# Zero borders in the background, pool waits tile by tile, a finer start of the first group, and NCA in longer pieces

## The chip, the core and the metric

The kernel runs on one core of a Trainium2 chip. A core has TensorE for matmuls (PE in the profile, with its weight loads as PEld), VectorE (DVE), ScalarE (ACT), GpSimd (POOL) and SyncE (SP); the last one only issues DMA transfers here, and ScalarE issues some too. Each engine works through its own instructions in a fixed order. The metric is the device time of one execution in microseconds.

## The reference, cut to what matters

The input x is 32 images of 8 channels and 256 x 256 points, in fp32. Two layers follow, each with a residual.

```python
# layer 0: on z = groupnorm(x), 4 groups of 2 channels
grid = z
for _ in range(15):                                  # the lattice
    mapped = 3.9 * grid * (1 - grid)
    grid = 0.85 * (0.7 * mapped + 0.3 * conv3x3_per_channel(mapped)) + 0.15 * z
cml = clip(grid, 1e-4, 1 - 1e-4)
nca = sigmoid(conv1x1(relu(conv3x3(z, 8 -> 128)), 128 -> 8))
g   = sigmoid(conv1x1(relu(conv3x3(concat(z, cml, nca), 24 -> 8))))
x   = x + g * cml + (1 - g) * nca
# layer 1: y = groupnorm(x); x = x + conv3x3 of y and the weights, both quantised to whole numbers up to 127;
# the scale of y is its largest magnitude over the whole batch
```

The lattice is a chain of 15 convolutions on one channel: a step needs the step before it, with the neighbouring rows. The quantisation of layer one needs all of layer zero, so the two layers can't overlap.

## The kernel before, in words

**Stages.** Layer zero is done in eight groups of four images (GB = 4, so NG = 8). Four kinds of work exist in it:

- *Preparation* (`normalise`): loads x by pairs of channels, takes means and variances, writes the normalised values to DRAM in two layouts: `xq_s` for the lattice, and `xp_s` for NCA, as a high and a low part (`hi`, `lo`). One tile is one image and one pair of channels (512 KB). The staging tiles `xq`, `hi` and `lo` exist once, so a tile waits until the stores of the one before it have read them.
- *Lattice* (`lattice`): one unit is one channel of the four images of a group, in two streams of two images. A unit has 15 steps, a step three tiles, a tile six matmuls (L486). After a tile VectorE computes L494 and L499 for each stream. After the second and third tile, two small DMAs (`exchange`, L449 and L450) carry edge rows of `m_a` to their neighbours, for the next step.
- *NCA* (`nca`): per image nine block pairs in two parts each, and a short rest. A part has four or three rounds of 12 matmuls into `ph` (L563), which ScalarE turns into `h` (L573); the products of `h` with the second weights (L580) are made one part later. Each part's input rows `im` are loaded one part ahead.
- *Gate* (`gate`): combines the results for an image of the group before and writes `y_s`.

**Order.** TensorE's order is written out by hand. The lattice is the main line: `together` lets it emit one step, and then emits filler (NCA, gate, preparation) until the filler's share has caught up. A piece of filler is what lies between two `yield`s, and the number given to `yield` is its weight in microseconds; a step weighs 5.91. The weights of whole stages are `T_NCA, T_GATE, T_PREP, T_LATTICE = 520.0, 340.0, 34.0, 8 * 45 * 1.97`. So filler is never cut within a piece, and the lattice never within a step. The other engines' orders are chosen by a planner that takes the program order as priority.

**DMA queues.** Nearly all transfers are issued from SP, in one fixed order. `background(n)` issues up to n waiting transfers of a list (`later`) after each lattice tile: the loads of the next unit and the stores of finished ones. Zero borders (rows above and below the images in `xp_s`, `cm_s`, `nc_s` and `y_s`) are written from ScalarE's queue in the preparation part, L199 and L202, from a zero tile `zt`.

**Memory.** The preparation part uses pools of its own for weights and for `zt`. The pools of layer zero (`xp` for the tiles of x, `hp` for `h`, and so on) take the same memory after them. A pool waits for all users of the memory that it takes over.

**The start.** `prep(0, (0,))` prepares two of the four channel groups for all four images of the first group ahead of the lattice, the other two as filler ahead of NCA.

Of the kernel before, what the change touches and what calls it, by code (L numbers as in the profile page):

```python
# [40 lines left out]
P = 128  # L41
# [72 lines left out]
def kernel(  # L114
# [19 lines left out]
    def dram_ap(t, offset, dims):  # L134
        return bass.AP(t.tensor, t.offset + offset, dims)
# [17 lines left out]
    qw = cp.tile([P, 3, P], BF16, name="qw")  # L153
    wp_hi = cp.tile([P, 3, HID], F32R, name="wp_hi")
    wp_lo = cp.tile([P, 3, HID], F32R, name="wp_lo")
    wu_z = cp.tile([HID, 56], F32, name="wu_z")
    bp_sb = cp.tile([P, 1], F32, name="bp_sb")
    bv = cp.tile([P, 4], F32, name="bv")
# [13 lines left out]
    with tc.tile_pool(name="prep", bufs=1) as pp, tc.tile_pool(name="prep2", bufs=2) as pp2:  # L172
# [18 lines left out]
        nc.sync.dma_start(bv, bvec)  # L191


        zt = pp.tile([P, PW], F32, name="zt")
        G.memset(zt, 0.0)
        for t, n, w in (
            *((t, 2 * C, PW) for t in xp_s), *((t, C, W) for t in (*cm_s, *nc_s, *y_s))
        ):
            nc.scalar.dma_start(dram_ap(t, 0, [[w, n], [1, w]]), zt[:n, :w])  # L199
            for i in range(0, 11, 5):  # L200
                m = min(5, 11 - i) * n
                nc.scalar.dma_start(dram_ap(t, (257 + i) * n * w, [[w, m], [1, w]]), zt[:m, :w])  # L202

        V.tensor_copy(masks, kt[:, K_MASK : K_MASK + 4])
        V.tensor_copy(junk, kt[:, K_JUNK : K_JUNK + 2])
# [51 lines left out]
    with ExitStack() as one:  # L257

        one.enter_context(tc.manual_schedule(engines={mybir.EngineType.PE}))
        pool = lambda name, bufs, **kw: one.enter_context(tc.tile_pool(name=name, bufs=bufs, **kw))  # L260
        xp, sp2, gp, bp2, st = pool("xp", 4), pool("sp2", 1), pool("gp", 3), pool("bp2", 2), pool("st", 2)
        imp, hp, wk, wk1, np_ = pool("imp", 3), pool("hp", 12), pool("wk", 2), pool("wk1", 1), pool("np", 1)
# [25 lines left out]
        def normalise(jobs):  # L288

            def begin(b, half):
# [3 lines left out]
                for i in range(2):  # L297
                    g = 2 * half + i
                    xr = xp.tile([P, 2, 2, W], F32, name="xr", tag="xr")
                    nc.sync.dma_start(  # L300
                        xr.rearrange("p c h w -> p (c h) w"),
                        dram_ap(x, (b * C + 2 * g) * H * W, [[W, P], [P * W, 4], [1, W]]),
                    )
                    for j in range(2):
                        V.bn_stats(stats[:, i, j, :], xr[:, j].rearrange("p h w -> p (h w)"))
                    V.bn_aggr(mv[:, i, :], stats[:, i].rearrange("p j s -> p (j s)"))
                    xrs.append(xr)
                return b, half, xrs, mv

            def scale(b, half, xrs, mv):  # L310
                gs = slice(2 * half, 2 * half + 2)
                pm = ps_c.tile([P, 512], F32, name="pm", tag="pt")
                T.matmul(pm[:, 0:2], avg, mv[:, :, 0], start=True, stop=True)
                m, rstd = mean_x[:, b, gs], rstd_x[:, b, gs]
                V.tensor_copy(m, pm[:, 0:2])
                e = st.tile([P, 2], F32, name="e", tag="e")
                V.tensor_tensor(e, mv[:, :, 0], m, ALU.subtract)
                V.tensor_tensor(e, e, e, ALU.mult)
                V.tensor_tensor(e, e, mv[:, :, 1], ALU.add)
                return e  # L320

            def end(b, half, xrs, e):
                pv = ps_c.tile([P, 512], F32, name="pv", tag="pt")
                T.matmul(pv[:, 0:2], avg, e, start=True, stop=True)
                rstd = rstd_x[:, b, 2 * half : 2 * half + 2]
                V.tensor_scalar(rstd, pv[:, 0:2], GN_EPS, None, ALU.add)
                G.tensor_tensor(rstd, rstd, mhalf[:, 0:2], ALU.pow)
                for i, xr in enumerate(xrs):
                    g = 2 * half + i
                    flat = xr.rearrange("p c h w -> p (c h w)")  # L330
                    V.tensor_scalar(
                        flat, flat, mean_x[:, b, g : g + 1], rstd_x[:, b, g : g + 1],
                        ALU.subtract, ALU.mult,
                    )
                    xq = sp2.tile([P, 2, 2, 4, NJ], F32, name="xq", tag="xq")
                    S.activation(
                        xq.rearrange("p c h q j -> p (c h) q j"),
                        xr.rearrange("p c h (j q) -> p (c h) q j", q=4),
                        AF.Copy,
                    )  # L340
                    inner = lambda t: t[:, :, :, 1 : 1 + W]
                    V.tensor_copy(inner(hi), xr)
                    G.tensor_tensor(inner(lo), xr, inner(hi).bitcast(F32), ALU.subtract)
                    for h in range(2):
                        nc.sync.dma_start(
                            dram_ap(
                                xq_s[b % NBUF], (2 * g * H + P * h) * W, [[W, P], [H * W, 2], [1, W]]
                            ),
                            xq[:, :, h].rearrange("p c q j -> p c (q j)"),
                        )  # L350
                        for j, src in enumerate((hi, lo)):
                            nc.sync.dma_start(
                                dram_ap(
                                    xp_s[b % NBUF],
                                    (1 + P * h) * ROW + (C * j + 2 * g) * PW,
                                    [[ROW, P], [PW, 2], [1, PW]],
                                ),
                                src.bitcast(F32)[:, :, h, :],
                            )
                    yield 1.0  # L360
                ready.add((b, half))
# [14 lines left out]
        def lattice(g):  # L376


            def load(u):


                c, out, dmas = u % C, [], []
                assert all((u // C * GB + i, c // 4) in ready for i in range(GB))
                for s in range(2):
                    i = (2 * u + s) % 4
                    da, db = d_a[i], d_b[i]
# [72 lines left out]
            for c in range(C):  # L459
                u = g * C + c  # L460
                ds = units[u]
                for step in range(STEPS):
# [5 lines left out]
                    for i, ts in enumerate(tiles):  # L468
# [46 lines left out]
                        if step == STEPS - 1 and u + 1 in units:  # L515
                            begin(units[u + 1], ts)

                        background(len(later) if (c, step, i) == (C - 1, STEPS - 1, 2) else 3)
                    yield 5.91

        ROWS = ((2, 4, 10, 12, 3, 5, 11, 13), (1, 6, 8, 14, 7, 9))
# [31 lines left out]
        def nca(b):  # L553
# [57 lines left out]
            for p in range(9):  # L611
                for part in range(2):
# [22 lines left out]
            if (b + 1, 0) in ready and (b + 1, 1) in ready:  # L635
                loaded[b + 1] = rows(b + 1, 0, 0)
            two = hidden([im[64 * q : 64 * q + 48, 0, :2, :] for q in range(2)])
            yield 1.4
# [225 lines left out]
        for _ in prep(0, (0,)):  # L864
            pass
        for g in range(NG):
            fill, t = images(nca, g), T_NCA
            if g:
                fill, t = both(fill, t, images(gate, g - 1), T_GATE), t + T_GATE
            if g + 1 < NG:  # L870
                fill, t = both(fill, t, prep(g + 1, (0, 1)), T_PREP), t + T_PREP
# [104 lines left out]
```

## Time and profile before

| | |
|---|---|
| time, median of 3 | 14845.17 us (14838.8 to 14852.71) |
| profiled execution | 14861.1 us, mean TensorE clock 0.946 |
| first load of x issued | 114.09 us |
| first step of lattice at full work | 217.97 us |
| groups 0, 1, 2 of the lattice begin | 199, 1675, 3339 us |
| end of the lattice | 13257 us |

The page lists busy time by engine, then the span in 40 slices of some 370 us each, where a digit is the busy share in tenths. PEclk is the clock granted to TensorE. Answers for a stretch of time give start, duration, engine, line, output and input of each instruction; in brackets stands how long the engine had been idle before it and what ended that.

### The profile page before, as it was taken

The numbers are of one execution on the slowest core, as the hardware profiler recorded it, in microseconds if no ns is written. First come the engines' busy times: TensorE is split into PE (matmuls) and PEld (weight loads), VectorE is DVE, ScalarE is ACT, GpSimd is POOL, SyncE is SP. The second block draws the span as 40 slices with busy tenths as digits, with TensorE's granted clock in tenths as the row PEclk, the third lists the DMA queues.
The fourth block names the chain that finished last, engine by engine and source line by source line (L and its number), as shares of the span: only waits on it lengthen the run. The fifth ranks groups of instructions, "written<-read, shape, count | busy, mean of one in ns | idle before, by whom it ended". The sixth has DMA issues, their size and how long they took to land.

```text
span 14861.1 us, 228715 instructions
## 1 busy us (share of the span) xinstructions
PE 13261.8 (89%) x81728; PEld 6416.2 (43%) x81728; DVE 8159.8 (55%) x16290; ACT 4040.8 (27%) x6274; POOL 2453.7 (17%) x4266
## 2 busy tenths in 40 slices
PE   2999999999999999999999999999999999997222
PEld 1545444444444444444444444444444444442010
DVE  3555555555555555555555555555555555555443
ACT  1333222322222222222222222223222222221121
POOL 1110111111111111111111111111111111123000
PEclk9999999999999999999999999999999999998565
DMA  5444434444444434444444444444444333333444
GB/s 147 94 100 96 100 89 101 104 105 96 99 101 99 112 90 97 107 104 99 97 99 101 109 96 97 106 104 97 101 101 103 85 84 83 78 81 100 125 127 115
DMA packets 2254946, 1496.67 MB, mean 101 GB/s; under 512 B 1056640, under 2 KB 2224896, under 8 KB 2253696
## 3 DMA queue, kind: packets, MB, share of 16 engines
q1 hardware_dynamic: 2243360, 1474.15, 42.1%
q8 instruction: 663, 10.86, 0.3%
q10 hardware_dynamic: 10464, 7.89, 0.2%
q14 instruction: 459, 3.76, 0.1%
HBM read 866.48 MB, written 478.69 MB: 91 GB/s over the span
## 4 chain that ended last, share of the span: by engine, by line
PE 73%; DVE 8%; SPq 7%; DMA 6%; issue 3%; POOL 1%; ACT 1%; ACTq 1%; DVEq 0%; POOLq 0%
PE pt L486 33%; PE ph L563 18%; PE pa L755 13%; PE acc L580 7%; SPq L927 4%; DVE gt L494 2%; PE pg L721 1%; DMA yb<-y_s 1%; DVE m_b L499 1%; DMA m_a<-m_a 1%; DMA im<-xp_s 1%; DVE qt L915 1%; DMA xb<-in_x_dram 1%; DMA xr<-in_x_dram 1%; DVE m_a L499 1%
## 5 line engine op out<-in xcount | busy, mean ns | idle before, releaser
L486 PE MATMUL pt<-m_a,lw 128*64 128x390 f32 x17280 | 5847.0, 497 | 162.1 <-DMA m_a<-m_a 116.7
L486 PE MATMUL pt<-m_b,lw 128*64 128x384 f32 x17280 | 5815.7, 492 | 22.8 <-DVE m_b L410 17.9
L573 ACT ACTIVATE h<-ph,bp_sb 128x512 f32<-128x512 f32 x4096 | 2581.0, 684 | 6255.2 <-PE ph L563 6183.3
L486 PEld LDWEIGHTS pt<-m_a,lw 128*64 128x64 f32 x17280 | 2308.7, 138 | 1823.3 <-issue 1670.9
L486 PEld LDWEIGHTS pt<-m_b,lw 128*64 128x64 f32 x17280 | 2312.5, 138 | 1602.4 <-issue 1469.8
L563 PE MATMUL ph<-im,wp_hi 48*128 48x512 f32 x12288 | 2718.3, 416 | 102.9 <-DMA im<-xp_s 54.9
L494 DVE SCALAR_TENSOR_TENSOR gt<-pt,d_b 128x390 f32<-128x390 f32 x2880 | 1606.8, 558 | 1824.7 <-PE pt L486 1821.6
L563 PE MATMUL ph<-im,wp_lo 48*128 48x512 f32 x12288 | 2603.4, 399 | 0.0
L494 DVE SCALAR_TENSOR_TENSOR gt<-pt,d_a 128x384 f32<-128x384 f32 x2880 | 1581.3, 549 | 1827.1 <-PE pt L486 1826.9
L503 POOL TENSOR_TENSOR m_b<-m_b,junk 128x12 f32<-128x12 f32 x2688 | 802.6, 299 | 8089.3 <-DVE m_b L499 7621.6
L563 PEld LDWEIGHTS ph<-im,wp_hi 48*128 48x128 f32 x12288 | 1334.8, 188 | 1015.0 <-DVE m_b L499 196.1
L499 DVE SCALAR_TENSOR_TENSOR m_b<-gt 128x390 f32<-128x390 f32 x2688 | 1559.9, 580 | 42.5 <-DVE gt L494 0.9
L499 DVE SCALAR_TENSOR_TENSOR m_a<-gt 128x384 f32<-128x384 f32 x2688 | 1518.4, 565 | 15.6
L563 PEld LDWEIGHTS ph<-im,wp_lo 48*128 48x128 f32 x12288 | 1330.5, 188 | 214.9
L580 PE MATMUL acc<-h,wu_z 128*32 128x512 f32 x8320 | 1173.3, 606 | 12.9 <-ACT h L573 7.4
L922 PE MATMUL pt<-qt,qw 128*128 128x512 bf16 (+1 forms) x960 | 291.1, 476 | 852.5 <-DVE qt L915 760.4
L755 PE MATMUL pa<-xnb,gw 128*64 128x512 f32 (+1 forms) x3840 | 892.9, 597 | 0.2
L755 PE MATMUL pa<-cmb,gw 128*64 128x512 f32 (+1 forms) x3840 | 852.8, 576 | 10.8 <-POOL cmb L677 10.8
L755 PE MATMUL pa<-nb,gw 128*64 128x512 f32 (+1 forms) x3840 | 849.6, 574 | 0.0
L726 POOL TENSOR_TENSOR d<-cmb,nb 128x512 f32<-128x512 f32 x320 | 511.5, 1598 | 1610.2 <-DVE gate L730 1428.5
L730 DVE TENSOR_TENSOR gate<-gate,d 128x512 f32<-128x512 f32 x320 | 216.2, 676 | 868.9 <-ACT gate L723 854.1
L767 ACT ACTIVATE r<-pa,bv 128x512 f32<-128x512 f32 x320 | 213.1, 666 | 1645.3 <-PE pa L755 1644.2
(132 smaller groups left out, 6964.1 us busy)
## 6 DMA issues: line engine op xcount, KB each, us to landing
im<-xp_s SPq DMA_DIRECT2D x1152, 193.5 KB
im<-xp_s SPq DMA_DIRECT2D x1216, 96.8 KB
yb<-y_s SPq DMA_DIRECT2D x32, 2432.0 KB
d_a<-xq_s SPq DMA_DIRECT2D x2048, 36.0 KB
nb<-nc_s SPq DMA_DIRECT2D x288, 256.0 KB
cq<-cm_s SPq DMA_DIRECT2D x288, 256.0 KB
xb<-in_x_dram SPq DMA_DIRECT2D x544, 128.0 KB
xp_s<-hi SPq DMA_DIRECT2D x256, 258.0 KB
```

The lines of the kernel that those rows point to most:

```text
L486: T.matmul(pt[half], lw[:, c, k, half], beside if part == 2 else own, start=part < 2, stop=part > 0,)
L494: V.scalar_tensor_tensor(gt, pt, FLOOR, d[:, ts, :], ALU.max, ALU.add)
L499: V.scalar_tensor_tensor(to, gt, 1.0, gt, ALU.subtract, ALU.mult)
L503: G.tensor_tensor(edge, edge, junk.unsqueeze(1).to_broadcast([P, 6, 2]), ALU.mult)
L563: T.matmul(ph[:, :n].rearrange("p (h w) -> p h w", w=W), w[64 * i : 64 * i + 48, dx, :], rhs[:, :, dx : dx + W], start=(dx == 0 and w is w ...
L573: S.activation(h[:, :n], ph[:, :n], AF.Relu, bias=bp_sb)
L580: T.matmul(acc[32 * g : 32 * g + 32, :cols], wu_z[:, 24 - 8 * i : 56 - 8 * i], h, start=first, stop=last,)
L726: G.tensor_tensor(three(d), cmb[:, :n, 1 : 1 + W], nin, ALU.subtract)
L730: V.tensor_tensor(y[:, :cols], gt[:, :cols], d[:, :cols], ALU.mult)
L755: T.matmul(three[half], gw[:, s * 3 + dx, half], t[:, :n, dx : dx + W], start=(i == 0), stop=(i == 8),)
L922: T.matmul(pt, qw[:, dx, :], q[:, k0 : k0 + n, dx : dx + W], start=(dx == 0), stop=(dx == 2))
L927: nc.sync.dma_start(dram_ap(out, b * C * H * W + (r - 1) * W, [[H * W, C], [STEP * W, n], [1, W]]), o[r * C : (r + 1) * C, :n, :],)
```

## The change

Four things are changed.

1. *Zero borders in the background.* Only the borders of the first four `xp_s` are written in the preparation part. All others go onto the list `later` and are issued from SP between lattice tiles, seven instead of three per tile in the first unit. `zt` is 64 columns wide, lives among the constants, and is repeated along a row, so a row is written in pieces of 64 numbers (43 for `xp_s`).
2. *Waits tile by tile.* The pools of layer zero wait for the memory of each tile alone (`reuse_waits="tile"`), and `hp`, which is used late, comes first, so that it takes the memory of the preparation part.
3. *A finer start.* The first group prepares one pair of channels ahead of the lattice, not two; then one, then two together.
4. *NCA in longer pieces.* A part is one piece of filler, of weight 7.6 or 6.2. Before, a part was two pieces.

The first three are meant to let the lattice start sooner; the last makes the interleaving coarser.

```diff
-        zt = pp.tile([P, PW], F32, name="zt")
         G.memset(zt, 0.0)
+        borders = []
         for t, n, w in (
-            *((t, 2 * C, PW) for t in xp_s), *((t, C, W) for t in (*cm_s, *nc_s, *y_s))
+            *((t, 2 * C, PW) for t in xp_s[:GB]),
+            *((t, C, W) for t in (*nc_s[:GB], *cm_s[:GB])),
+            *((t, 2 * C, PW) for t in xp_s[GB:]),
+            *((t, C, W) for t in (*nc_s[GB:], *cm_s[GB:], *y_s)),
         ):
-            nc.scalar.dma_start(dram_ap(t, 0, [[w, n], [1, w]]), zt[:n, :w])
...
+            k = 64 if w == W else 43
+            for row, m in ((0, 1), (257, 5), (262, 5), (267, 1)):
+                borders.append(
...
+        for _ in range(4 * GB):
+            nc.scalar.dma_start(*borders.pop(0))
...
-        pool = lambda name, bufs, **kw: one.enter_context(tc.tile_pool(name=name, bufs=bufs, **kw))
-        xp, sp2, gp, bp2, st = pool("xp", 4), pool("sp2", 1), pool("gp", 3), pool("bp2", 2), pool("st", 2)
+        pool = lambda name, bufs, **kw: one.enter_context(
+            tc.tile_pool(name=name, bufs=bufs, reuse_waits="tile", **kw)
+        )
+        hp, xp, sp2, gp, bp2 = pool("hp", 12), pool("xp", 4), pool("sp2", 1), pool("gp", 3), pool("bp2", 2)
...
-                        background(len(later) if (c, step, i) == (C - 1, STEPS - 1, 2) else 3)
+                        background(len(later) if (c, step, i) == (C - 1, STEPS - 1, 2) else 3 if u else 7)
...
                             done = drain()
                             pend = None
-                            yield 4.8
-                        elif i == 1 or i == 3 - part:
-                            yield 1.4 * (i % 2 + 1)
+                    yield 7.6 - 1.4 * part
...
-        def prep(g, halves):
-            return normalise([(b, half) for half in halves for b in range(g * GB, g * GB + GB)])
+        def prep(g, groups=((0, 1), (2, 3))):
+            return normalise([(b, gs) for gs in groups for b in range(g * GB, g * GB + GB)])
...
-        units, later = {}, []
+        units, later = {}, borders
...
-        for _ in prep(0, (0,)):
+        for _ in prep(0, ((0,),)):
             pass
...
             if g == 0:
-                fill, t = chain(prep(0, (1,)), fill), t + 20.0
+                fill, t = chain(prep(0, ((1,), (2, 3))), fill), t + 30.0
```

More of the change, by code (lines that the diff above doesn't have):

```diff
@@ L155 @@
     wp_lo = cp.tile([P, 3, HID], F32R, name="wp_lo")
+    zt = cp.tile([P, 64], F32, name="zt")
     wu_z = cp.tile([HID, 56], F32, name="wu_z")
@@ L191 @@
         nc.sync.dma_start(bv, bvec)
-        zt = pp.tile([P, PW], F32, name="zt")
         G.memset(zt, 0.0)
+        borders = []
         for t, n, w in (
-            *((t, 2 * C, PW) for t in xp_s), *((t, C, W) for t in (*cm_s, *nc_s, *y_s))
-        ):
-            nc.scalar.dma_start(dram_ap(t, 0, [[w, n], [1, w]]), zt[:n, :w])
-            for i in range(0, 11, 5):
-                m = min(5, 11 - i) * n
-                nc.scalar.dma_start(dram_ap(t, (257 + i) * n * w, [[w, m], [1, w]]), zt[:m, :w])
+            *((t, 2 * C, PW) for t in xp_s[:GB]),
+            *((t, C, W) for t in (*nc_s[:GB], *cm_s[:GB])),
+            *((t, 2 * C, PW) for t in xp_s[GB:]),
+            *((t, C, W) for t in (*nc_s[GB:], *cm_s[GB:], *y_s)),
+        ):
+            k = 64 if w == W else 43
+            for row, m in ((0, 1), (257, 5), (262, 5), (267, 1)):
+                borders.append(
+                    (
+                        dram_ap(t, row * n * w, [[w, m * n], [k, w // k], [1, k]]),
+                        zt[: m * n, :k].unsqueeze(1).to_broadcast([m * n, w // k, k]),
+                    )
+                )
+        for _ in range(4 * GB):
+            nc.scalar.dma_start(*borders.pop(0))
         V.tensor_copy(masks, kt[:, K_MASK : K_MASK + 4])
@@ L259 @@
         one.enter_context(tc.manual_schedule(engines={mybir.EngineType.PE}))
-        pool = lambda name, bufs, **kw: one.enter_context(tc.tile_pool(name=name, bufs=bufs, **kw))
-        xp, sp2, gp, bp2, st = pool("xp", 4), pool("sp2", 1), pool("gp", 3), pool("bp2", 2), pool("st", 2)
-        imp, hp, wk, wk1, np_ = pool("imp", 3), pool("hp", 12), pool("wk", 2), pool("wk1", 1), pool("np", 1)
+        pool = lambda name, bufs, **kw: one.enter_context(
+            tc.tile_pool(name=name, bufs=bufs, reuse_waits="tile", **kw)
+        )
+        hp, xp, sp2, gp, bp2 = pool("hp", 12), pool("xp", 4), pool("sp2", 1), pool("gp", 3), pool("bp2", 2)
+        st, imp, wk, wk1, np_ = pool("st", 2), pool("imp", 3), pool("wk", 2), pool("wk1", 1), pool("np", 1)
         ps_c, ps_a = pool("ps_c", 6, space=PSUM), pool("ps_a", 2, space=PSUM)
@@ L288, in normalise, with begin @@
         def normalise(jobs):
-            def begin(b, half):
+            def begin(b, gs):
                 xrs = []
@@ L296, in begin @@
                 stats = st.tile([P, 2, 2, 6], F32, name="stats", tag="stats")
-                for i in range(2):
-                    g = 2 * half + i
+                for i, g in enumerate(gs):
                     xr = xp.tile([P, 2, 2, W], F32, name="xr", tag="xr")
@@ L307, in begin, with scale, end @@
                     xrs.append(xr)
-                return b, half, xrs, mv
-            def scale(b, half, xrs, mv):
-                gs = slice(2 * half, 2 * half + 2)
+                return b, gs, xrs, mv
+            def scale(b, gs, xrs, mv):
+                n = len(gs)
+                m = mean_x[:, b, gs[0] : gs[0] + n]
                 pm = ps_c.tile([P, 512], F32, name="pm", tag="pt")
[L313 to L317, printed above, removed]
+                T.matmul(pm[:, 0:n], avg, mv[:, :n, 0], start=True, stop=True)
+                V.tensor_copy(m, pm[:, 0:n])
+                e = st.tile([P, 2], F32, name="e", tag="e")[:, :n]
+                V.tensor_tensor(e, mv[:, :n, 0], m, ALU.subtract)
                 V.tensor_tensor(e, e, e, ALU.mult)
-                V.tensor_tensor(e, e, mv[:, :, 1], ALU.add)
+                V.tensor_tensor(e, e, mv[:, :n, 1], ALU.add)
                 return e
-            def end(b, half, xrs, e):
+            def end(b, gs, xrs, e):
+                n = len(gs)
                 pv = ps_c.tile([P, 512], F32, name="pv", tag="pt")
[L324 to L329, printed above, removed]
+                T.matmul(pv[:, 0:n], avg, e, start=True, stop=True)
+                rstd = rstd_x[:, b, gs[0] : gs[0] + n]
+                V.tensor_scalar(rstd, pv[:, 0:n], GN_EPS, None, ALU.add)
+                G.tensor_tensor(rstd, rstd, mhalf[:, 0:n], ALU.pow)
+                for g, xr in zip(gs, xrs):
                     flat = xr.rearrange("p c h w -> p (c h w)")
@@ L359, in end @@
                             )
+                    ready.add((b, g))
                     yield 1.0
-                ready.add((b, half))
             ahead = None
@@ L382, in load @@
                 c, out, dmas = u % C, [], []
-                assert all((u // C * GB + i, c // 4) in ready for i in range(GB))
+                assert all((u // C * GB + i, c // 2) in ready for i in range(GB))
                 for s in range(2):
@@ L634, in nca @@
             im = ahead
-            if (b + 1, 0) in ready and (b + 1, 1) in ready:
+            if all((b + 1, g) in ready for g in range(4)):
                 loaded[b + 1] = rows(b + 1, 0, 0)
@@ L870 @@
             if g + 1 < NG:
-                fill, t = both(fill, t, prep(g + 1, (0, 1)), T_PREP), t + T_PREP
+                fill, t = both(fill, t, prep(g + 1), T_PREP), t + T_PREP
             if g == 0:
-                fill, t = chain(prep(0, (1,)), fill), t + 20.0
+                fill, t = chain(prep(0, ((1,), (2, 3))), fill), t + 30.0
             together(lattice(g), T_LATTICE, fill, t)
```

## The prediction, made before the changed kernel was run

> **What bounds the kernel now.** I read the slices of the page first, then the table of stretches, then the opening minute by minute, then the waits of TensorE.
>
> ```profile
> PE 13261.8 (89%) x81728; PEld 6416.2 (43%) x81728; DVE 8159.8 (55%) x16290; ACT 4040.8 (27%) x6274; POOL 2453.7 (17%) x4266
> PE   2999999999999999999999999999999999997222
> PEclk9999999999999999999999999999999999998565
> ```
> ```profile
> 218.00:310.00 92.00, 36.94 (x159) 17.54 (x159) 56.13 (x128) 18.62 (x14) 25.30 (x24) 0.68 0.67 194
> 420.00:1675.00 1255.00, 1184.70 (x7626) 622.52 (x7624) 698.56 (x1436) 387.40 (x605) 130.97 (x322) 0.96 0.44 97
> 3339.00:5004.00 1665.00, 1620.09 (x10099) 785.15 (x10098) 949.51 (x2000) 477.59 (x744) 306.49 (x528) 0.98 0.43 101
> ```
> Columns of the second view: stretch, length, busy PE, PEld, DVE, ACT, POOL, granted clock, DMA share, GB/s. TensorE is full from 420 us on; a group of four images (3339 to 5004) is 97% busy at clock 0.98. So time goes only where TensorE has nothing, in the opening and in layer two (which the change leaves alone), and every new hole in the middle counts in full.
>
> The opening:
> ```profile
> 111.97 1.04 ACTq L202 DMA_DIRECT2D y_s<-zt  x3
> 114.09 2.06 SPq L300 DMA_DIRECT2D xr<-in_x_dram  x4
> 118.17 1.29 DVE L305 BATCH_NORM_STATS2 stats<-xr 128x6 f32<-128x512 f32 x2 [85.33 <-DMA xr<-in_x_dram]
> 126.76 2.08 ACT L336 ACTIVATE xq<-xr 128x1024 f32<-128x1024 f32 x1 [7.33 <-DVE xr L331]
> 185.75 2.03 ACT L336 ACTIVATE xq<-xr 128x1024 f32<-128x1024 f32 x1 [6.37 <-DMA xq_s<-xq]
> 217.97 1.55 PE L486 MATMUL pt<-m_b,lw 128*64 128x384 f32 x4 [17.90 <-DVE m_b L410]
> ```
> VectorE stands 85 us because the first loads of x leave only when the last border has been written. Then eight tiles pass, 8.4 us each ((185.75 - 126.76)/7), and the lattice runs from 218 us. It crawls while the other eight tiles pass (9.1 us each, ACT's L336 from 233.30 to 296.84); NCA starts here:
> ```profile
> 310.65 0.76 PE L563 MATMUL ph<-im,wp_hi 48*128 48x512 f32 x1 [10.07 <-DMA im<-xp_s]
> ```
> The waits inside the full stretch:
> ```profile
> PE pt L486 <- DMA m_a<-m_a: 116.7, 43, 8.7
> ```
> ```profile
> 1600.08 0.51 PE L486 MATMUL pt<-m_a,lw 128*64 128x390 f32 x1 [2.39 <-DMA m_a<-m_a]
> 1647.55 0.89 PE L486 MATMUL pt<-m_a,lw 128*64 128x390 f32 x1 [6.42 <-DMA m_a<-m_a]
> ```
> Both are starts of a lattice step with no NCA or gate work ahead of it. A step is 5.85 us of matmuls; its rows for the next step leave by L449/L450 once VectorE has done the second tile (5.6 to 5.9 us after the step's start), take 1.2 us to issue and over 1 us to land. Filler hides this; without filler TensorE stands.
>
> **What the skill says.** "TensorE: Matmul & The Clock Gate", What's actually happening: an idle window of about 3.4 us halves the clock, and a busy window restores it. The trace agrees in kind but is harsher: after holes of 1.64 and 0.49 us at 550 us,
> ```profile
> 541.00:551.00 10.00, 8.93 (x62) 4.13 (x54) 6.46 (x16) 1.37 (x3) 0.62 (x3) 1.00 0.99 160
> 552.00:562.00 10.00, 9.51 (x38) 4.96 (x39) 0.00 (x0) 3.45 (x7) 0.00 (x0) 0.50 0.37 97
> ```
> the next ten ran at 0.50. "DMA: Bandwidth & Descriptors", Issuing engines are not separate DMA queues: moving a DMA to another queue moves only its issue time. The trace has that price: 0.31 to 0.47 us for a border on ACT's queue, 0.43 for a d_a load of 144 pieces on SP's. Same page, Why small descriptors are slow (HBM only): pieces of 256 bytes and less carry overhead; borders go to pieces of 256 and 172 bytes. Their 7.9 MB beside 1497 MB leave this small. "Perfetto Trace Analysis", Identifying the Most-Contended Engine: TensorE's busy share is no distance to its roof. I therefore use it only to place holes.
>
> **The change, part by part.**
>
> *Borders and pools.* The loads of x need no border any more. With zt among the constants, waits taken tile by tile and hp first in memory, xr overlaps no preparation tile. Statistics can start when VectorE is nearly done with the weights (28 us, still mixed with about 7 us of small weight work). In the run before, the first hi cast came 9.2 us after the first statistics; with the mixing I take 15, so 43 us instead of 127.4: -84.
>
> *First group one channel pair at a time.* Four tiles instead of eight ahead of the lattice: 4 x 8.4 = -34. The lattice's full start goes from 218 to 100 us.
>
> *Given back.* Twelve tiles instead of eight then stand between lattice start and NCA: 4 x 9.1 = +36. About 105 of the 256 borders left stand on SP's queue among them (counted in the instruction order of the built program): 105 x 0.45 = 47 us of issue. In 218:310 that queue issued for 39 of 92 us, so some fits. I take +25, bounds 0 and 47. Queued behind them are xq_s and xp_s stores, for which the next tile waits. NCA starts near 310.65 - 118 + 36 + 25 = 254 us. By then six lattice steps are done instead of four, 2 x 5.85 = -12. Sum of the opening: -57 - 12 = -69.
>
> *Other borders.* About 130 leave in steps 6 to 14 of the first unit, seven per tile, 58 us of issue on a queue that was 0.53 to 0.61 busy (63.3 of 120 us from 310; 104 of 170 from 430). The exchanges L449/L450 queue behind them and TensorE waits for those. +20, bounds 0 and 40.
>
> *NCA in longer pieces.* The work is the same and so, within two per group, is the count of changes between kinds of matmul; nothing is saved. What moves is where it stands. In group 0 a lattice step earns 5.91 x (520 + 34 + 30)/709 = 4.87 units of filler. Pieces were 4.8, 2.8, 4.8 and 1.4; they become 7.6 and 6.2. Two pieces (13.8) now pay for 2.8 steps, so nearly one step in three follows its predecessor bare. Counted in TensorE's built order: group 0, after the sixth step, 39 steps with under 1 us of filler instead of 6, none with 1 to 2 instead of 5. Groups 1 to 6 (7.45 units a step, gate pieces between): 3 under 1 us and one of 1.28 instead of none; group 7: one and one.
>
> Cost of a bare step, from the trace: step period less 5.85 us, its filler, and the usual overhead of that filler (0.14 per us of NCA, 0.23 per change of kind, fitted over undisturbed steps). The six bare steps of group 0 cost 27 us together, 4.5 each (2.7 at least; 7.6 where the half clock followed); steps with 1.28 us cost 3.5; with 2.56 nothing. Bounds of the bare cost: 2.5 (idle alone) and 6.5 (that idle and about 8 us of half clock).
> Group 0: 39 x 4.5 - (27 + 16 paid now) = +133 (54 to 210). Groups 1 to 7: 19 x 4.5 + 7 x 3.5 = +110 (57 to 160).
>
> Sum: -69 + 20 + 133 + 110 = +194, so 14845 + 194 = 15,040 us.
>
> **Rivals.**
> *Idle alone.* The bare step costs 2.5 us and no clock: -69 + 20 + 54 + 57 = +62, 14,907. For it: the hole of 2.39 us at 1600 left the clock at 1.00. Against: most holes of 2 to 3 us in group 0 were followed by half clock.
> *Faster: longer pieces also close holes.* Beside bare steps, group 0 now loses 69 us over that usual overhead to holes after late im loads and full PSUM (after 420 us, bare and 1.28 us steps left out), and each later group some 20, together 209. If longer pieces closed all of these and SP's queue held, the sum is 194 - 209 - 20 = -35, and with no extra for borders in the crawl -60: 14,785. For it: the holes at 550 and 601 us are of this kind. Against: im is asked for one part ahead as before, and a part follows it no later; nothing in the trace says that the cuts between pieces cause the holes.
> *The queue chokes.* SP's in-order queue makes both border terms their upper bounds and spoils the crawl further: +22 + 20 and some 40 more, 15,120. For it: 0.88 issue share at 200:218 already. Against: 0.43 in the crawl.
>
> **How the numbers follow.** Forecast 0.48, idle alone 0.20, faster 0.17, choked queue 0.15. Faster than 14,815 us comes from the third case: 0.16. Within 0.2%: 0.06, between the second and third. Slower: 0.78. All low bounds together give 14845 - 94 + 0 + 54 + 57 = 14,862, all high ones 14845 - 47 + 40 + 210 + 160 = 15,208. Both at once are unlikely; I cut the top a little and stretch the low end toward the faster case: 14,825 to 15,170.
>
> **What would show it.** Loads of xr near 16 us; first full lattice step near 100; NCA near 254. Group 0 ending at 1675 - 69 + 20 + 133, about 1760. Waits of the lattice on m_a up from 117 us to 200 or more, and clock below 0.96 in group 0. Groups 1 to 6 some 17 us longer than 1665. Wrong if bare steps cost under 2 us, if the holes after im vanish, or if NCA starts after 300 us.

## The result, and the profile after

The changed kernel takes 15036.17 us, median of 4 runs (15021.59 to 15045.97); the kernel before, beside it, 14846.83 us (14838.8 to 14852.71). The ratio is 1.0127, 95% interval 1.011 to 1.0145. Line numbers after L200 are 11 to 13 higher than before: the lattice matmul L486 is L499, `background`'s transfers L444 are L457, `ph` L563 is L576.

The page of the changed kernel, answering to the lines shown of before:

```profile
PE 13314.5 (89%) x81744; PEld 6601.2 (44%) x81744; DVE 8204.6 (55%) x16310; ACT 4038.9 (27%) x6274; POOL 2469.0 (16%) x4270
PE   3899899999999999999999999999999999997222
PEclk7999999999999999999999999999999999998656
```

TensorE's busy time rose by 53 us, its span by 183. The first slice went from 2 to 3 only, and the second and the sixth from 9 to 8: the lattice starts earlier, but not at full work.

The opening in the timeline (start, duration, engine, line, output and input; in brackets the idle time before and what ended it):

```profile
41.63 2.05 ACT L349 ACTIVATE xq<-xr 128x1024 f32<-128x1024 f32 x1 [15.68 <-DVE xr L344]
190.60 2.06 ACT L349 ACTIVATE xq<-xr 128x1024 f32<-128x1024 f32 x1 [42.39 <-DVE xr L344]
222.31 5.42 SPq L457 DMA_DIRECT2D nc_s<-zt  x7
289.19 2.04 ACT L349 ACTIVATE xq<-xr 128x1024 f32<-128x1024 f32 x1 [20.98 <-DMA xq_s<-xq]
301.33 0.76 PE L576 MATMUL ph<-im,wp_hi 48*128 48x512 f32 x1 [44.37 <-DMA im<-xp_s]
```

The first tile is ready at 41.6 us as forecast (126.76 before), and a full lattice step runs at 102. But ScalarE gets its twelfth tile beside the lattice only at 289 us: (289.19 - 112.05)/11 = 16.1 us a tile, where 8.4 to 9.1 was seen before. The cause stands in the third line: seven borders occupy SP's queue for 5.42 us. Stores that the next tile waits for are queued behind such runs. NCA starts at 301, 9 us earlier than before, not 57.

The waits of TensorE over the whole span (engine and tile, what it waited for, total us, times, longest):

```profile
PE pt L499 <- DMA m_a<-m_a: 245.2, 110, 14.5
```

It was 116.7 us in 43 waits. Now the span in four stretches. "Step 20" is the moment at which 20 lattice steps are done, when the borders have left and both kernels have done nearly equal filler (608 and 548 matmuls of NCA, some 7 us apart). Groups 1 to 7 are counted to the start of the last lattice step:

| us, from the traces | to step 20 | rest of group 0 | groups 1 to 7 | after the lattice |
|---|---|---|---|---|
| before | 494 | 1181 | 11,577 | 1610 |
| after | 547 | 1234 | 11,652 | 1612 |
| difference | +53 | +53 | +75 | +2 |
| prediction | -27 | +111 | +110 | 0 |

The prediction's -49 and +133 are moved to these columns: of the 39 bare steps that it counts (lattice steps with under 1 us of filler behind them), 6 are done before step 20, 5 more than before, so 22 us of the 133 belong to the first column. The total was right, and each of its three terms was off by 35 to 80 us. The experiments ask why.

### The profile page after: what moved, and what is told of

Read it like the earlier page. It is cut to its first block, busy times and chain, and to the rows that moved or that the text cites. A ratio compares the mean times of both kernels' runs of the same rounds, so it can differ in the third digit from the quotient of the medians.

```text
span 15044.2 us, 229231 instructions
## 1 busy us (share of the span) xinstructions
PE 13314.5 (89%) x81744; PEld 6601.2 (44%) x81744; DVE 8204.6 (55%) x16310; ACT 4038.9 (27%) x6274; POOL 2469.0 (16%) x4270
## 4 chain that ended last, share of the span: by engine, by line
PE 69%; SPq 8%; DVE 8%; DMA 7%; issue 3%; POOL 2%; ACT 1%; POOLq 0%; DVEq 0%; ACTq 0%
PE pt L499 32%; PE ph L576 18%; PE pa L766 12%; PE acc L593 6%; SPq L938 4%; DVE gt L507 2%; DMA m_a<-m_a 1%; DMA im<-xp_s 1%; PE pg L732 1%; SPq L457 1%; DMA yb<-y_s 1%; DVE m_b L512 1%; DVE m_a L512 1%; DVE qt L926 1%; DMA xb<-in_x_dram 1%
## 5 line engine op out<-in xcount | busy, mean ns | idle before, releaser
L499 PE MATMUL pt<-m_a,lw 128*64 128x390 f32 x17280 | 5798.8, 500 | 340.6 <-DMA m_a<-m_a 245.2
L499 PE MATMUL pt<-m_b,lw 128*64 128x384 f32 x17280 | 5754.6, 494 | 44.5 <-ACT h L586 23.1
L499 PEld LDWEIGHTS pt<-m_a,lw 128*64 128x64 f32 x17280 | 2257.7, 138 | 1837.2 <-issue 1398.3
L499 PEld LDWEIGHTS pt<-m_b,lw 128*64 128x64 f32 x17280 | 2278.5, 138 | 1598.4 <-issue 1381.5
L576 PE MATMUL ph<-im,wp_hi 48*128 48x512 f32 x12288 | 2671.3, 418 | 128.5 <-DMA im<-xp_s 68.0
L576 PE MATMUL ph<-im,wp_lo 48*128 48x512 f32 x12288 | 2535.0, 397 | 0.0
L576 PEld LDWEIGHTS ph<-im,wp_hi 48*128 48x128 f32 x12288 | 1263.1, 187 | 1243.8 <-issue 479.7
L576 PEld LDWEIGHTS ph<-im,wp_lo 48*128 48x128 f32 x12288 | 1262.4, 188 | 219.7
L707 DVE TENSOR_SCALAR xnb<-xb,sc 128x256 f32<-128x256 f32 x608 | 268.8, 458 | 637.3 <-DMA xb<-in_x_dram 577.9
```

What stands on the lines that cost most here:

```text
L499: T.matmul(pt[half], lw[:, c, k, half], beside if part == 2 else own, start=part < 2, stop=part > 0,)
L576: T.matmul(ph[:, :n].rearrange("p (h w) -> p h w", w=W), w[64 * i : 64 * i + 48, dx, :], rhs[:, :, dx : dx + W], start=(dx == 0 and w is w ...
L707: V.tensor_scalar(xnb[:, k, 1 : 1 + W], xb[:, k, :], sc[:, i : i + 1], sc[:, 1:2], ALU.subtract, ALU.mult,)
```

## The experiments

Each ran beside the kernel before on the same chip, where that took 14,858 to 14,872 us; so ratios to it are compared. A ratio's interval is about 0.0013 to either side, and 0.001 is 15 us. The labels stand in the headings below.

| run | ratio | to step 20 | rest of group 0 | groups 1 to 7 |
|---|---|---|---|---|
| after | 1.0127 | 547 | 1234 | 11,652 |
| e1: old pieces | 1.0041 | 555 | 1180 | 11,589 |
| e2: before, long pieces | 1.0122 | 519 | 1240 | 11,671 |
| e3: borders spread | 1.0080 | 425 | 1272 | 11,690 |
| e5: both e1 and e3 | 0.9969 | 420 | 1198 | 11,597 |
| e6: e5, old start | 0.9972 | 414 | 1216 | 11,567 |
| e7: borders by rows | 1.0123 | 458 | 1235 | 11,726 |
| e8: e5, finer pieces | 0.9986 | 417 | 1187 | 11,615 |
| e9: warm bare steps | 1.0130 | 550 | 1226 | 11,676 |
| e10: e6, zeros in DRAM | 0.9956 | 411 | 1194 | 11,577 |
| e11: e3, no exchange | 0.9804 | 392 | 1085 | 11,490 |
| e12: e5, no exchange | 0.9867 | 400 | 1081 | 11,583 |
| e13: e10, sums apart | 0.9831 | 413 | 1196 | 11,397 |

### The pieces: e1_old_pieces and e2_long_pieces_alone

```diff
-                    yield 7.6 - 1.4 * part
+                            yield 4.8
+                        elif i == 1 or i == 3 - part:
+                            yield 1.4 * (i % 2 + 1)
```

e2 makes the opposite edit on the kernel before.

> The changed kernel, but NCA again in its old pieces (4.8, 2.8, 4.8 and 1.4); pools, borders and the finer start stay. Theory (two losses: bare lattice steps cost some 45 us net in group 0 and 75 us in groups 1 to 7; the rest, about 100 us against the prediction, is border DMAs ahead of the exchanges on SP's queue in the first unit): 14,915 us, 120 less than after; from step 20 on 14 instead of 34 steps of group 0 with under 2 us of filler, groups 1 to 6 back near 1665 us, NCA still starting near 300 us. Rival A (the pieces cost nothing net, the queue is all): 15,035. Rival B (the pieces are the whole loss): 14,845 or less.

> The kernel before with only the longer NCA pieces; its borders all on ACT's queue ahead of everything, its old start. Theory: 14,847 + 45 + 75 = 14,965 us; group 0 about 45 us longer, groups 1 to 7 some 75 us together; NCA starts at 310 us as before. Rival A: 14,850. Rival B: 15,035 or more.

Measured: 1.0041 (1.0028 to 1.0054), so the old pieces give back 0.0086, 128 us; and 1.0122 (1.0109 to 1.0136) for long pieces alone, 181 us. Both say that the pieces cost; for e2 the theory had 120. e1 says that they are not the whole loss. e2 alone doesn't say so: its interval takes in the 1.0127 of the whole change, as rival B had it. So the losses don't add (0.0122 and 0.0041 against 0.0127), and the price of the pieces is higher where no borders stand in the queue. In e2 25 us of it fall before step 20 (519 against 494 us).

### The borders: e3_spread_borders, e5_old_pieces_spread, e7_row_borders

e3 and e5 keep the borders on a list of their own:

```diff
-        units, later = {}, borders
+        units, later = {}, []
...
-                        background(len(later) if (c, step, i) == (C - 1, STEPS - 1, 2) else 3 if u else 7)
+                        background(len(later) if (c, step, i) == (C - 1, STEPS - 1, 2) else 3)
+                        if u and (step + i) % 2 == 0 and borders:
+                            nc.sync.dma_start(*borders.pop(0))
```

> The changed kernel, long pieces kept, but its 256 borders are on a list of their own and leave one at a time, every second lattice tile, from the second unit of group 0 to the fourth of group 2, instead of three to seven per tile ahead of everything else in the first unit. Theory: NCA starts near 254 us as predicted, the twelve prep tiles pass at about 9.1 us each instead of 16.1, and the time falls by about 100 us, to 14,935. Rival A (the queue is all): 14,845 or less. Rival B (prep tiles are slow for their own sake, borders hide): 15,035, tiles still at 16 us.

> Both edits on the changed kernel: old pieces and borders spread one at a time. Theory, if the two losses add: 15,036 - 120 - 100 = 14,815 us, under the kernel before by 30; NCA from about 254 us. If they overlap (holes after im that the long pieces had closed come back, and hide borders' waits too): 14,850 to 14,900. If the finer start is worth all that was predicted for it (69 + 25 us): 14,755.

Measured: 1.0080 (1.0067 to 1.0094) and 0.9969 (0.9956 to 0.9981). In e5 NCA starts 55 us earlier than in after:

```profile
245.84 0.76 PE L578 MATMUL ph<-im,wp_hi 48*128 48x512 f32 x1 [30.89 <-DMA im<-xp_s]
```

The prediction's sum without its 25 us for borders gives 229 us. The twelve tiles beside the lattice pass at 10.7 us each here, not at 9.1, which is about the difference; so of the 16.1 us a tile in after, the borders are to blame for 5.4.

Step 20 comes 122 us earlier in e3 than in after, 135 earlier in e5 than in e1. Not all of it lasts: the whole difference is 70 us with long pieces and 107 with old ones, and the rest of group 0 is longer (e3 1272, after 1234). Probably that is because the same DMAs must still be issued later, where they also stand in somebody's way; no run tests this by itself.

Why is a border so dear? The list of instructions by tile gives DMA issue times (count; shortest, median, longest in ns; first and last start). In the kernel before, on ACT's queue:

```profile
L202 ACTq DMA_DIRECT2D y_s<-zt x96: 279/310/648, 67.1 to 112.7; - x96
L199 ACTq DMA_DIRECT2D y_s<-zt x32: 306/307/307, 66.8 to 111.6; - x32
```

In the kernel after, on SP's and on ACT's:

```profile
L457 SPq DMA_DIRECT2D y_s<-zt x128: 660/764/1077, 304.9 to 437.3; - x128
L457 SPq DMA_DIRECT2D xp_s<-zt x32: 562/622/1105, 119.1 to 175.2; - x32
L213 ACTq DMA_DIRECT2D xp_s<-zt x16: 569/626/888, 1.0 to 22.3; - x16
```

The borders of `xp_s` take 0.62 us on either queue, so the queue is not the reason. The number of pieces matters little: of y's borders those with 32 pieces (8 partitions by 4) took 0.67 us and those with 160 pieces 0.78 us, in medians; before, 8 and up to 40 whole rows took the same 0.31. What is left is the form, a short tile repeated along each row. e7 changes that form alone, repeat and length of the pieces at once (and `xb` from three buffers to two, to make room; only the gate uses it):

```diff
-    zt = cp.tile([P, 64], F32, name="zt")
+    zt = cp.tile([P, PW], F32, name="zt")
...
-            k = 64 if w == W else 43
+            k = w
```

> The changed kernel with its borders cut into whole rows of 1 KB (zt again as wide as a row, no repeat of a 64-number piece); same places, same number of DMAs, same queue, same order. To make room xb has two buffers instead of three, which only the gate uses, from group 1 on, so group 0 is what is to be read. Theory (the time of the queue is what costs): a border issues in 0.31 to 0.43 us as on ACT's queue in the kernel before, not 0.62 to 0.78; some 256 x 0.4 = 100 us of issue less, of which 0.65 reach TensorE: step 20 of the lattice at about 480 instead of 547 us, NCA from about 275 instead of 301, group 1 from about 1,715 instead of 1,781. Rival (it is the bytes and pieces at the DMA engines, or the count of DMAs): step 20 near 547, NCA near 300.

```profile
L457 SPq DMA_DIRECT2D y_s<-zt x128: 263/297/1666, 261.4 to 349.8; - x128
L457 SPq DMA_DIRECT2D xp_s<-zt x32: 302/424/717, 32.5 to 150.0; - x32
```

Issue falls to 0.30 us (0.42 for `xp_s`), step 20 from 547 to 458 us and group 1's start from 1781 to 1694. That is more than expected (480 and 1,715). The count of DMAs is out as a rival, for count and places are the same. Longer pieces could also have eased the DMA engines, but these were not the limit: their busy share from 102 us to the start of NCA is 0.57 in after and 0.65 in e5, where the tiles pass faster. The ratio, 1.0123, shows nothing of the gain, because the gate with two buffers, the only other thing that e7 changes, takes it back: groups 1 to 7 are 74 us longer, and the gate of the last group, after the lattice, 26.

### The finer start: e6_old_start

```diff
-        for _ in prep(0, ((0,),)):
+        for _ in prep(0, ((0, 1),)):
...
-                fill, t = chain(prep(0, ((1,), (2, 3))), fill), t + 30.0
+                fill, t = chain(prep(0, ((2, 3),)), fill), t + 20.0
```

> The run with old pieces and spread borders, but with the old start: both tiles of the first channel pairs of all four images (eight tiles) are normalised ahead of the lattice, the other eight beside it. Pools that wait by tile, borders and pieces as in that run. Theory, from the first full step of the kernel before (218 us) less the 84 us that the loads came earlier: lattice full at about 134 instead of 102 us, then eight tiles instead of twelve before NCA, which starts near 227 instead of 252 us; step 20 at about 412 against 420, so the total is the same within 10 us: the finer start earns nothing. Rival (the finer start is worth the 34 us of its four tiles): 34 us slower, 14,860.

Measured: 0.9972 (0.9961 to 0.9982) against 0.9969 for e5. NCA starts at 219.5 instead of 245.8 us, step 20 at 414 instead of 420. The finer start earns nothing that can be seen: twelve tiles instead of eight then stand ahead of NCA.

### Wait or clock: e9_warm_bare_steps

A bare step of the changed kernel, in the timeline of TensorE (the step starts at 697.49, right behind the one before):

```profile
697.16 0.49 PE L499 MATMUL pt<-m_b,lw 128*64 128x384 f32 x1
...
697.49 0.81 PE L499 MATMUL pt<-m_b,lw 128*64 128x384 f32 x2
700.32 0.88 PE L499 MATMUL pt<-m_a,lw 128*64 128x390 f32 x4 [2.03 <-DMA m_a<-m_a]
...
701.87 0.86 PE L499 MATMUL pt<-m_a,lw 128*64 128x390 f32 x1
```

The stream that works on `m_b` needs no rows and goes ahead; the other waits 2.03 us for its edge rows. A single matmul then takes 0.86 us, ahead of the hole 0.49: the clock has halved. From the start of its first matmul to that of its last the step takes 10.1 us instead of 5.6. e9 fills such steps (`bare` is true where `together` emitted no piece):

```diff
+                if bare:
+                    idle = ps_c.tile([P, 512], F32, name="idle", tag="pt")
+                    for _ in range(15):
+                        T.matmul(
+                            idle[:, :384], wp_hi[:48, 0, :], wp_hi[:48].rearrange("p a b -> p (a b)"),
+                            start=True, stop=True,
+                        )
```

> The changed kernel with 15 matmuls that compute nothing of use (2.4 us) behind each lattice step of any group that gets no piece of filler; their result is not read. They do not shorten the wait for the edge rows, they only keep TensorE at work through it. Bare steps of group 0 after step 20: 33 to 6. If the 4.3 us of a bare step are 2.4 us of wait plus about 2 us of half clock: 28 x 1.9 = about 50 us less in group 0 and 20 in later groups, 14,970. If they are wait alone: 15,036 or a little more. If the half clock comes from something else than these holes: 15,036 with as much half clock as before (99 us in group 0 after step 20).

The rest of group 0 in the table of stretches (length, busy PE, PEld, DVE, ACT, POOL, granted clock, DMA share, GB/s), after:

```profile
547.00:1781.00 1234.00, 1123.51 (x7196) 593.10 (x7196) 653.38 (x1344) 367.88 (x574) 120.62 (x301) 0.96 0.43 93
```

and with warm bare steps:

```profile
550.00:1776.00 1226.00, 1174.24 (x7616) 638.42 (x7616) 652.88 (x1345) 367.77 (x575) 120.24 (x301) 0.98 0.43 94
```

The time at half speed fell, from 2 x 0.04 x 1234 = 99 to about 50 us, and the length of the stretch by 8 us; the ratio is 1.0130 (1.0116 to 1.0144), no gain. The split of a bare step can be read from the traces: by the prediction's own sum the 33 bare steps of after cost 142 us, 4.3 each. In them lie 92 us of waits of over 0.15 us, 2.8 a step, and 82 us at half clock, in 19 of the 33, which cost half of that, 1.2 a step. So the expected split, 2.4 and 2, was near. What my expectation of 50 us less left out is the price of the filler. The same step in e9:

```profile
699.75 2.87 PE L849 MATMUL idle<-wp_hi 48*128 48x384 f32 x15
```

The fifteen matmuls hold TensorE for 2.9 us where the hole was 2.03. In 20 of the 28 filled steps no wait is left, so the filler is longer than what it fills, and costs about as much as hole and half clock together. Shorter filler was not tried.

### What the wait is: e11_no_exchange_long and e12_no_exchange_old

```diff
-                                    exchange(m_a[s], k)
+                                    pass
```

> The run with long pieces and spread borders, without the exchange of edge rows between the tiles of the lattice: the two transfers m_a to m_a per half and step are left out (3,584 in all), so that the edge rows of each tile keep their own values and the output is not the reference's. Theory (a bare step waits for these rows and for little else): the 33 bare steps of group 0 after step 20 cost under 1.5 us each instead of 5.0, group 0 falls by some 120 us after step 20, and SP's issue time falls by 3,584 x 0.6 = 2,150 us, which may close other holes too: below 14,850. Rival (a bare step waits for VectorE's own chain or runs at half clock for another reason): they still cost 3 us or more.

> The run with old pieces and spread borders, equally without the exchange of edge rows. It gives the price of the long pieces when no step waits for rows: with the exchange they cost 165 us (ratios 1.008 and 0.9969). Theory: without it the difference between the two runs shrinks to 40 us or less. Rival (long pieces cost something else, PSUM or im or the order of kinds of matmuls): it stays above 100 us.

Measured: 0.9804 (0.979 to 0.9817) with long pieces, 0.9867 (0.9854 to 0.9881) with old ones. The 33 bare steps cost 0.0 us each instead of 5.0. The stretch from step 20 to the end of group 0, with long pieces and spread borders:

```profile
425.00:1697.00 1272.00, 1137.45 (x7194) 601.08 (x7192) 649.39 (x1335) 367.55 (x574) 120.09 (x300) 0.94 0.42 92
```

and the same without exchange:

```profile
392.00:1477.00 1085.00, 1071.10 (x7194) 558.33 (x7192) 637.83 (x1331) 366.89 (x574) 119.93 (x300) 0.99 0.47 99
```

The holes are gone, and the half clock with them. And the sign of the long pieces turns: 165 us slower with the exchange (1.0080 against 0.9969), 94 us faster without. So they have a gain of their own, and the edge rows turn it into a loss; neither the theory (40 us or less) nor its rival had that. By stretches, the exchange costs 187 us in the rest of group 0 and 200 us in groups 1 to 7 with long pieces, but 117 and only 14 with old ones. That the bare steps cost nothing now shows the edge rows as their cause. One reservation on the rest: without the exchange SP issues 3,584 DMAs less (0.57 to 0.59 us each), so not all of the time gained need be the wait for rows.

The gain shows in the waits of groups 1 to 7. Before:

```profile
PE pm L788 <- DVE dv L805: 88.3, 20, 4.6
PE pt L486 <- DMA m_a<-m_a: 71.1, 23, 8.7
```

After:

```profile
PE pt L499 <- DMA m_a<-m_a: 103.0, 70, 11.2
PE pt L499 <- ACT h L586: 59.7, 24, 3.7
PE ph L576 <- DVE gt L507: 46.6, 36, 5.7
PE pm L799 <- DVE dv L816: 31.9, 7, 4.6
```

`pm` is the small sum at the end of the gate of an image: mean, then variance of y, each waiting for VectorE. Long pieces put other work between, 56 us less; e3 against e5 and e11 against e12, where the pieces alone differ, show the same (31.9 against 88.3, and 31.9 against 87.5). What they cost there is 32 us on edge rows, 60 us of lattice steps that wait for ScalarE to read `h`, and 24 us more on VectorE's `gt` (46.6 after, 22.8 before); +59 in all, of the 75 measured. The wait on `h` fits the buffers: a piece now takes six or eight `ph` in a row from a pool of six that it shares with the lattice, four before.

### Better versions: e8_finer_pieces, e10_zeros_from_dram, e13_gate_sums_apart

e8 cuts NCA once more than the old pieces do:

```diff
                             pend = None
-                            yield 4.8
-                        elif i == 1 or i == 3 - part:
-                            yield 1.4 * (i % 2 + 1)
+                            yield 2.0
+                        yield 1.4
```

> The run with old pieces and spread borders, with NCA cut once more: a piece ends after each pair of block rows (1.4), the products for themselves (2.0). After step 20 of group 0 five steps with under 2 us of filler instead of 14. Theory (what counts is how evenly filler lies between lattice steps): about 25 us less in group 0, nothing after it, 14,800. Rival (holes wait on im and PSUM, cuts do not matter, or more cuts make more waits): 14,825 or more.

Measured: 0.9986 (0.9977 to 0.9994) against 0.9969 (0.9956 to 0.9981), so by the medians 25 us slower where 25 faster was expected; the intervals just touch. Group 0 did get 11 us shorter after step 20, but groups 1 to 7 got 18 us longer. There TensorE changes between kinds of work 342 times more often; at the 0.23 us a change from the prediction's fit that is an estimate of 79 us, against 53 us less of waits of over 0.15 us (258 for 311). No run tests this explanation.

```diff
+        zd = dp.tile([80, PW], F32, name="zd")
+        nc.scalar.dma_start(dram_ap(zd, 0, [[PW, 80], [1, PW]]), zt[:80])
...
-                        dram_ap(t, row * n * w, [[w, m * n], [k, w // k], [1, k]]),
-                        zt[: m * n, :k].unsqueeze(1).to_broadcast([m * n, w // k, k]),
+                        dram_ap(t, row * n * w, [[w, m * n], [1, w]]),
+                        dram_ap(zd, 0, [[w, m * n], [1, w]]),
```

> The run with old pieces, spread borders and old start, but with the zeros in DRAM: one 80-row array is written once from ACT's queue, and every border is a copy of its first rows, whole rows on both sides; zt goes back to the preparation. Same places, number, queues and order of the borders. Theory (the form of the transfer sets its issue time): a border issues in 0.30 to 0.35 us instead of 0.74, 240 x 0.4 = 96 us of SP's time less in groups 0 to 2; spread as they are, few stood in the way, so 10 to 30 us less: 14,795. Rival (the spread borders are hidden already): 14,815.

```profile
L534 SPq DMA_DIRECT2D y_s<-zd x128: 468/540/1810, 1360.8 to 2443.9; - x128
```

Measured: 0.9956 (0.9942 to 0.9969). Issue fell to 0.54 us only, not to 0.31: whole rows are not enough when the source is in DRAM too. The 24 us lie inside the expectation, but the intervals of e6 and e10 overlap.

```diff
-            yield 0.5
+            yield 3.0
             V.tensor_copy(m, total(ma[:, 0:1], mb[:, 0:1]))
...
-            yield 0.5
+            yield 3.0
             V.tensor_scalar(rstd, total(e[:, 0:1], e[:, 1:2]), GN_EPS, None, ALU.add)
```

> The run with zeros from DRAM, and the two pieces at the end of the gate of an image (mean, then variance of y, each a small sum on TensorE that waits for VectorE) marked 3.0 instead of 0.5 long, so that a whole lattice step or part of one comes between them. Theory (long NCA pieces moved other work between these two sums: TensorE waited 31.9 us on them with long pieces and 88.3 with old ones): the wait falls from 88 to about 30 us without any bare step more than two, 50 us less: 14,755, ratio 0.992. Rival (those waits are on no path that counts, or move elsewhere): no change, 0.9956.

Measured: 14618.65 us, ratio 0.9831 (0.9818 to 0.9845): 186 us less than e10, not 50, and the fastest complete version. The waits of TensorE in groups 1 to 7, e10 first:

```profile
PE pm L804 <- DVE dv L821: 88.3, 20, 4.6
PE pt L500 <- DMA m_a<-m_a: 71.2, 31, 7.7
```

```profile
PE ph L579 <- DVE gt L508: 48.1, 78, 2.7
PE pt L500 <- DMA m_a<-m_a: 21.0, 21, 8.6
```

The 88.3 us are off the list (its smallest shown entry is 11.6), and edge rows cost 50 us less too. In e10 a stretch at half clock goes with each of the 20 waits, 160 us in all, which costs up to 80 more; with these waits it is gone. All in all the waits of over 0.15 us in groups 1 to 7 fall from 303 to 174 us and the time at half clock from 382 to 188, worth 97: together 226 where the stretch got 180 shorter, so the two overlap.

Not all of this belongs to the sums. 37 of the 50 us on edge rows are five waits of 7.2 to 7.7 us, each some 20 us before the end of a group, with no sum near. Heavier pieces move the other filler as well, and these five went with that. By an estimate from these numbers, 186 - 37 = 149 us are left for 88 us of waits: with the half clock behind them they cost over one and a half times their length, and my estimate of 50 us counted only part of their length.

## Why the prediction was right, and where it was not

**Loads and first tile.** Right: 41.6 us for 43, full lattice step 102 for 100.

**Borders on SP's queue.** Wrong, in size. The counts were right to the piece (105 before NCA, 130 after it in the first unit); their issue was taken at 0.45 us from rows on ACT's queue, and is 74.4 us / 105 = 0.71 and 95.6 / 130 = 0.74. The prediction saw that the pieces get smaller and looked only at bytes; the kernel before has no repeated tile from which the price could have been read. Also "some fits" was too kind: step 20 came 122 us later than with spread borders (e3), where +25 and +20 were taken and 47 and 40 were the upper bounds. This is the rival of the choked queue, and it ate the opening: with the borders out of the way, step 20 stands 69 us (e3) to 74 us (e5) earlier than before, and 72 is what the prediction's sum gives for e3 without its border terms.

**Finer start.** Taken as -34, +36 and -12. Their sum, -10, is too small for e6 to show (0.9972 against 0.9969, with intervals of about 0.001).

**Bare steps in group 0.** Right in size, 4.3 us for 4.5, in the cause, the edge rows (e11: 0.0), and in taking both wait and clock: 2.8 and 1.2 us. "Idle alone, 2.5 us" leaves out the clock, which halved in 19 of the 33 steps. The Trainium skill, "TensorE: Matmul & The Clock Gate", What's actually happening, ties the half clock to an idle window of about 3.4 us; here a hole of 2.03 us has it behind it, and it is the smaller part, 41 of 142 us.

**Other holes.** Wrong. The prediction gave "longer pieces close holes" a chance of 0.17 and nothing in the sum. In the rest of group 0 the time lost outside bare steps, by the prediction's fit, fell from 73 to 10 us, which is most of why +111 became +53. The traces show it as waits of over 0.15 us (53, then 19) and as time at half clock (89, then 14). e2, with long pieces alone, has 33 and 38, so the pieces did most of it. The argument against it ("nothing in the trace says that the cuts between pieces cause the holes") looked at `im` alone, whose waits went only from 7.3 to 5.1 us; those of NCA on VectorE's `gt` went from 13.9 to 2.7. Nor were the `pm` sums of the later groups looked at, 88.3 us in the waits of before.

**Groups 1 to 7.** +75 for +110; the sign "some 17 us longer" a group came true with 15. The 19 bare and 7 short steps cost 40 and 8 us instead of 85 and 25: a bare step costs 2.1 us there, less than half the 4.5 carried over from group 0. In their place came the wait on `h`, which the prediction did not have, less the 56 us at `pm`.

So 15,040 was met by luck: errors of +80, -58 and -35 us nearly cancel. Of its three signs of being wrong, one came true, NCA after 300 us, and one in part: the holes of group 0 went, but those after `im` are not among them.

What stays open: how much of e11's gain is SP's freed queue, how e13's gain splits between the sums and the filler that moved, and whether filler no longer than the hole would have paid in e9.

## What to carry to other kernels

A DMA put "in the background" of an in-order queue costs its issue time to everything queued behind it, so measure that time in the form in which it will be issued before moving it, and spread what moves. Filler for a chain that waits on a fixed latency must lie behind every link: count the links that get none, and price one from the trace. Before filling a hole with work that computes nothing, compare the two lengths: 2.9 us in holes of 2.0 us and a little more gained nothing here. Before coarsening or refining pieces, look through the waits for short sums that bounce between engines; here two numbers in their order gained 186 us, about what the whole change lost.

## What the runs showed of the hardware that was not expected

- The issue of a DMA depends on its form more than on its size: 0.30 to 0.31 us for whole 1 KB rows from a tile; 0.67 us on 8 and 0.78 us on 40 partitions when a 64-number piece is repeated along the row; 0.54 us from DRAM to DRAM.
- A hole of 2.03 us was enough for half clock behind it; 19 of 33 steps with such holes (2.8 us of waits on average) had it. Filling them with 2.9 us of useless matmuls halved the time at half clock (99 to 50 us) and gained 8 us of 1234. Where 88 us of waits were taken away and not filled, 160 us at half clock went with them.
